# Reordering the last spans of each layer in a two-layer graph network kernel: late edge rows added by VectorE from SBUF, slot sums in one portion, block sums ahead of older blocks' stages, source one-hots earlier

## The chip, the cores and the metric

The kernel runs on one core of a Trainium2 chip. The metric is the device time of one execution in microseconds (us). Three runs of the kernel before took 2167.27, 2167.39 and 2170.34 us; their median is 2167.39.

## What is computed

Two graph layers over 6250 nodes and 106250 edges, rows of 256 float32. The edges are sorted by target node. Cut to what matters:

```python
# layer 0
msg = relu(x[src] + edge_attr)
h = 2 * x + segment_sum(msg, dst)
f = gelu(bn1(h) @ W1.T + b1) @ W2.T + b2
x1 = layernorm(x + bn2(h + f))
# layer 1
m = gelu((x1[src] + edge_attr) @ W1m + b1m) @ W2m + b2m
agg = segment_sum(m, dst) / max(deg, 1)
u = gelu(agg @ W1u + b1u) @ W2u + b2u
out = layernorm(x1 + layernorm(x1 + u) * gamma + beta)
```

The kernel adds 2x into a block's sum as a product with twice the identity. Layer 0's first product and layer 1's last message product work on block sums. Layer 1 gathers rows of `proj = x1 @ W1m + b1m`, so that the product with W1m is made once for each node, and once for each edge's own row.

## The kernel before

**Spans.** The edges are cut into 831 tiles of 128, and the tiles into 104 spans (0 to 103) of 8 (two groups of 4; a *quad* or pair is two tiles). For each span POOL gathers the source rows, one indirect DMA a tile (`gather`, L829), into one of five ring buffers. VectorE (DVE) adds the edge rows into the ring (`add_to_gathered`, L884), ScalarE (ACT) applies relu or gelu (L892, for pairs L898). TensorE (PE) then sums a span's edges into 128 *slots*: one-hots of the slot (L907, `one_hots`) times the rows, a PSUM bank named slotP of which there is one (L927, `slots_of`; `into_slots` does all 8 tiles, interleaved over four column groups). ACT copies the sums to SBUF (L946, `kept_slots`), and PE adds them into the node blocks they belong to (L966, `into_blocks`, with the degrees at L974).

**Blocks.** Node blocks have 256 nodes, and the last two 128 and 96; call them X and Y, and the last wide one A. When a block's last span has been added, its stages begin as a Python generator, one stage for each `advance`. In layer 0 (`nodes_0`) they are: copies out of the sum (begun by `full_0`); the first product (L1029) and gelu; the second product (L1042, L1047), the residual (L1052, L1054) and the statistics; square root (L1002), reciprocal (L1003) and scale (L1007), with the write of x1; transposes (L1066); the product with W1m (L1075, L1079) and the write of proj (L1084, for X and Y L1086). In layer 1 (`nodes_1`): residuals (L1331, L1335), the mean, the first product in two halves (L1357, L1362, L1367), the second product (L1378, L1382), a first norm (L1388, L1392) and the last norm with the write of the result. All use one PSUM bank named nodeP. `further()` advances every block that is running by one stage.

**Order.** The program is under a manual schedule: every engine runs its instructions in the order in which the Python code issues them, and waits for its operands there. So the order of calls in `step_0`, `step_1`, `late_step`, `end_0` and `end_1` is the order on each queue, the DMA queues of SP and POOL among them. `step_0(v)` gathers span v, adds the edge rows of span v-1 (first copied by ACT into PSUM, `lifted`, L867), and sums span v-2 into slots; `full_0(v-3)` adds the sums of span v-3 into blocks. The last four spans of each layer (100 to 103) go through `late_step` and `summed`. There the edge rows come to PSUM by PE, as products with an identity (`raised`, L875, 16 matmuls a span), and the slot sums are made in four portions of two tiles, with calls of `further()` between them.

**The turn.** Layer 1 can't gather from blocks that layer 0 hasn't finished. Its first three spans (AHEAD = 3; 24 gathers, from `src_near`) take only the rows of blocks up to A, and a blank row for a source in X or Y; all later gathers read the whole of proj. What the first three spans miss is put in by one-hots of the source: `where(i)` loads a copy of four tiles' source numbers to all partitions by a broadcast DMA (L1242, 256 KB) and compares them (DVE, L1250), and `completed` multiplies them with the rows of X and Y (PE, L1262). `added(v)` adds the first spans' edge part.

**The functions around the change** (`end_0` closes layer 0, `end_1` layer 1; before them `step_0` or `step_1` runs for spans 0 to 100, after `end_0` `step_1` begins):

Of the kernel before, what the change touches and what calls it, by code (L numbers as in the profile page):

```python
# [11 lines left out]
AF = mybir.ActivationFunctionType  # L12
# [3 lines left out]
D = 256  # L16
KC = D // P
G = 4
# [487 lines left out]
def kernel(  # L506
# [17 lines left out]
    nc = tc.nc  # L524
# [14 lines left out]
    ident = consts.tile([P, P], F32)  # L539
# [20 lines left out]
    col, at = {}, 0  # L560
    for name, n in COLS:
# [28 lines left out]
        ident=ident, ones=ones, eps=eps, col=col, row=row, src_sb=src_sb, dstf=dstf,  # L590
# [12 lines left out]
    V = len(window)  # L603
# [27 lines left out]
    def tiles_of(v, g):  # L631

        t0 = v * SPAN + g * G
        return [min(P, E - t * P) for t in range(t0, min(T, t0 + G))]

    def runs(counts):

        j = 0
        while j < len(counts):
            k = j  # L640
            while k < len(counts) and counts[k] == counts[j]:
                k += 1
            yield j, k, counts[j]
            j = k
# [3 lines left out]
    with (  # L648
# [17 lines left out]
        def work():  # L666
            return psw.tile([P, 2, D], F32, name="workP")
# [199 lines left out]
                nc.scalar.copy(ps[:n, j:k, :], of[:n, q + j : q + k, :])  # L867
            return ps

        def raised(v, g, q, of):  # L870

            pair = tiles_of(v, g)[q : q + 2]
            ps = work()
            for j, n in enumerate(pair):
                nc.tensor.matmul(  # L875
                    ps[:n, j, :], lhsT=ident[:n, :n], rhs=of[:n, q + j, :], start=True, stop=True
                )
            return ps

        def add_to_gathered(v, g, q, ps):  # L880
            at = g * G + q
            r = rings[v % RING]
            for j, k, n in runs(tiles_of(v, g)[q : q + 2]):
                nc.vector.tensor_add(  # L884
                    r[:n, at + j : at + k, :D], ps[:n, j:k, :], r[:n, at + j : at + k, :D]
                )
# [7 lines left out]
        def activated_pair(v, g, q, func):  # L894
            at = g * G + q
            for j, k, n in runs(tiles_of(v, g)[q : q + 2]):
                r = rings[v % RING][:n, at + j : at + k, :D]
                nc.scalar.activation(r, r, func)  # L898
# [37 lines left out]
        def into_slots(v, width):  # L936

            ps = slot_bank()
            count = len(tiles_of(v, 0) + tiles_of(v, 1))
            slots_of(v, width, ps, [j for i in range(PAIR) for j in range(i, count, PAIR)])  # L940
            return ps

        def kept_slots(v, ps, width):
            del hots[v]
            kept = hp.tile([P, D + 1], F32, name="sums")
            nc.scalar.copy(kept[:, :width], ps[:, :width])  # L946
            sums[v] = kept, ps
# [34 lines left out]
        running = []  # L982
# [106 lines left out]
        farther = []  # L1089
        eas, xbs, acc, degs = {}, {}, {}, {}  # L1090
# [68 lines left out]

        QUADS = [(g, q) for g in range(GROUPS) for q in range(0, G, 2)]  # L1160

        def summed(v, width, func, between=lambda i: None):

            one_hots(v)
            slot_nodes(v)
            its = [i for i in QUADS if tiles_of(v, i[0])[i[1] :]]
            rows = [raised(v, g, q, eas[v, g]) for g, q in its]
            for (g, q), ps in zip(its, rows):
                add_to_gathered(v, g, q, ps)
                activated_pair(v, g, q, func)  # L1170
            ps = slot_bank()
            for i, (g, q) in enumerate(its):
                between(i)
                at = g * G + q
                slots_of(v, width, ps, range(at, at + len(tiles_of(v, g)[q : q + 2])))
            kept_slots(v, ps, width)

        def further():
            advance(list(running))

        def late_step(v, full, func, width):

            u = v - 1
            if v == V - LATE:
                full(u - 2)
                activated(u - 1, 1, func)
                slot_nodes(u - 1)
                kept_slots(u - 1, into_slots(u - 1, width), width)
                further()
                full(u - 1)  # L1190
            summed(u, width, func, lambda i: further() if i % 2 else None)
            further()
            full(u)

        def kept_of(v):

# [38 lines left out]
        def added(v):  # L1235
            for g, q in QUADS:
                add_to_gathered(v, g, q, lifted(v, g, q, eas[v, g]))

        def where(i):

            to = check.tile([P, T], F32, name=("tiles", "off")[i % 2])[:, : G * P]
            nc.sync.dma_start(  # L1242
                out=to,
                in_=src_rows[i * G : (i + 1) * G, :].rearrange("t e -> (t e)")[None, :]
                .to_broadcast([P, G * P]),
            )
            hot = ep.tile([P, G, D], F32, name="z", bufs=2).rearrange("p g d -> p (g d)")
            hot = hot.rearrange("p (b e) -> p b e", e=G * P)
            for b in range(len(LAST)):
                nc.vector.tensor_scalar(  # L1250
                    hot[:, b, :], to, -float(near + sum(LAST[:b])), place,
                    op0=ALU.add, op1=ALU.is_equal,
                )
            wheres.append(hot)
# [13 lines left out]
        def end_0():  # L1268

            d = V - 1  # L1270
            for v in range(V - LATE, V):
                gather(v, x, src_sb)
                late_step(v, full_0, AF.Relu, D + 1)
            other = list(running)[-1]
            assert len(running) == 1 and len(farther) == 0
            for v in range(AHEAD):
                gather(v, proj[: near + 1, :], src_near)
                load_1(v)
            summed(d, D + 1, AF.Relu, lambda i: further() if i % 2 == 0 else None)
            full_0(d, acc_work)  # L1280
            last = list(running)[-1]
            assert len(running) == 2
            advance([last])
            for i in (0, 1):
                where(i)
            for _ in range(3):
                advance([other])
                advance([last])
            added(0)
            further()  # L1290
            further()
            assert not running and len(farther) == len(LAST)
            added(1)


# [156 lines left out]
        def full_1(v, bank=node_work, last=False):  # L1452
            for b in into_blocks(v, acc_1, opened_1):
                if last:
                    gen = prepared.pop(b)
                else:
                    gen = nodes_1(b, acc_1[b], x1s.pop(b), degs_1.pop(b), invs.pop(b), bank, last)
                del acc_1[b]
                begun(b, gen)
            invert()  # L1460
# [44 lines left out]
        def end_1():  # L1505

            d = V - 1
            for v in range(V - LATE, V):
                gather(v, proj, src_1)
                if v == V - 1:  # L1510
                    for b, bank in zip(sorted(acc_1), (node_work, acc_work)):
                        prepare(b, bank)
                late_step(v, lambda u: full_1(u, last=u == d - 1), AF.Gelu, D)
            assert len(running) == 1
            other = running[0]
            summed(d, D, AF.Gelu, lambda i: further() if i < 3 else None)
            full_1(d, last=True)
            last = running[-1]
            advance([last])
            advance([last])  # L1520
            while running:
                advance(list(running))
# [23 lines left out]
    other = nc.values_load(astray_i[:1, :1], min_val=0, max_val=2 * P)  # L1546
# [57 lines left out]
```

## Time and profile before

| What | Value |
|---|---|
| median of the runs shown | 2167.39 us (2167.27 to 2170.34) |
| the profiled execution | 2165.82 us, of which span 2163.9 us |
| mean granted TensorE clock | 0.968 |
| busy: PE, DVE, ACT, POOL | 1903.9, 1451.8, 1341.3, 1583.8 us |
| stretch 1010 to 1064: PE, DVE, ACT, POOL busy | 49.74, 27.61, 21.06, 30.11 of 54.00 us |
| stretch 2080 to 2160: PE, DVE, ACT, POOL busy | 59.01, 45.84, 33.13, 26.35 of 80.00 us |
| last gather of layer 0 ends | 1047.1 us |
| write of A's rows of proj issued (L1084) | 1058.85 us |
| first gather of layer 1 / first from the whole of proj | 1061.84 / 1094.94 us |
| identity groups (L875) start, layer 0 | 1020.73, 1035.61, 1049.64, 1061.01 us |
| identity groups (L875) start, layer 1 | 2086.67, 2099.76, 2120.15, 2133.50 us |
| block sums (L966) of spans 100 to 103 start, layer 1 | 2098.78, 2117.30, 2132.40, 2146.93 us |

The times are from one execution, taken by the hardware profiler, counted from the span's start. PEclk is the share of its full clock that TensorE was granted. A timeline row gives the start, the duration, the engine, the line and the operation, and in brackets how long the engine had been idle before, and what ended that. The chain of waits is the work that ended last, followed back from the last instruction to what released it. A row of a windows table gives for one stretch the busy time of each engine, the number of its instructions in parentheses, the granted clock, the DMA engines' share and the rate.

### The profile page before, as it was taken

To read this page: it belongs to the slowest core of one execution; us is meant where nothing else is said; L and a number is where in the kernel's file an instruction comes from. 1 tells how busy PE (TensorE), PEld (TensorE's weight loads), DVE (VectorE), ACT (ScalarE), POOL (GpSimd) and SP (SyncE) were. 2 spreads that over 40 slices of the span, in tenths; PEclk is the share of its full clock that TensorE was granted. 3 is DMA by queue.
4 is the path that set the end of the run, shared out by engine and by line. 5 is a ranking of instruction groups with operands and counts; after the bars stand their busy time and mean duration, and the time that the engine had idled before them with its cause. 6 is when DMAs were issued, how large, how long until landed. Compare 5 with 4: busy or idle time off the path is not lost.

```text
span 2163.9 us, 38059 instructions
## 1 busy us (share of the span) xinstructions
PE 1903.9 (88%) x12071; PEld 1472.0 (68%) x12071; DVE 1451.8 (67%) x4205; ACT 1341.3 (62%) x2153; POOL 1583.8 (73%) x1671
## 2 busy tenths in 40 slices
PE   5999999998998989898779998898888988888886
PEld 3777767776776777666557776677766766766654
DVE  6677766776776667666366766676676766666665
ACT  3577766676766666665336766665665666666653
POOL 7777777777777777777567777777777777777770
PEclk9999999999999999999989999999999999999998
DMA  9889888888988898887568777777777767777650
GB/s 335 263 290 323 293 294 290 292 287 286 301 289 283 287 295 281 286 288 243 174 206 267 225 244 233 221 238 243 227 227 228 242 213 235 219 233 227 212 167 26
DMA packets 318430, 541.75 MB, mean 250 GB/s; under 512 B 37260, under 2 KB 234125, under 8 KB 318093
## 3 DMA queue, kind: packets, MB, share of 16 engines
q1 hardware_dynamic: 237773, 319.65, 44.3%
q0 software_dynamic: 79744, 217.71, 32.6%
q8 instruction: 99, 1.62, 0.3%
q10 hardware_dynamic: 704, 1.87, 0.2%
q14 instruction: 110, 0.90, 0.1%
HBM read 461.90 MB, written 77.18 MB: 249 GB/s over the span
## 4 chain that ended last, share of the span: by engine, by line
PE 21%; DMA 12%; DVE 8%; issue 6%; ACT 4%; POOL 3%; DVEq 0%; ACTq 0%; POOLq 0%
DMA ring<-proj,dst_sb 11%; PE workP L856 8%; POOL ring L829 3%; PE slotP L927 3%; DVE ring L884 2%; PE nodeP L1378 2%; PE acc L966 2%; PE nodeP L1357 2%; DVE hot L907 2%; PE workP L843 1%; DVE uT L1362 1%; ACT ring L892 1%; ACT L1002 1%; PE workP L1262 1%; ACT workP L867 1%
## 5 line engine op out<-in xcount | busy, mean ns | idle before, releaser
L829 POOL DMA_INDIRECT ring<-in_x_dram,src_sb x831 | 789.0, 949 | 255.6 <-issue 137.3
L829 POOL DMA_INDIRECT ring<-proj,dst_sb x807 | 769.9, 954 | 252.8 <-issue 152.3
L856 PE MATMUL workP<-w1m_sb,eaT 128*128 128x256 f32 x3324 | 830.0, 395 | 67.8 <-DVE ring L884 45.4
L884 DVE TENSOR_TENSOR ring<-workP,ring 128x512 f32<-128x512 f32 x844 | 557.2, 684 | 426.8 <-DMA ring<-in_x_dram,src_sb 126.0
L856 PEld LDWEIGHTS workP<-w1m_sb,eaT 128*128 128x128 f32 x3324 | 621.1, 195 | 237.2 <-DVE ring L884 58.3
L892 ACT ACTIVATE ring<-ring 128x1024 f32<-128x1024 f32 x400 | 424.8, 1062 | 147.7 <-DVE ring L884 144.7
L848 ACT COPY eaT<-workP 128x512 f32<-128x512 f32 x416 | 223.8, 585 | 262.7 <-PE workP L843 261.6
L867 ACT COPY workP<-ea 128x512 f32<-128x512 f32 x606 | 334.0, 595 | 32.0 <-DVE ring L884 30.6
L966 PE MATMUL acc<-hot,sums 128*128 128x161 f32 (+22 forms) x1376 | 225.1, 296 | 91.5 <-DVE hot L960 48.9
L907 DVE TENSOR_SCALAR hot<-ramp,slot 128x32 f32<-128x32 f32 x1662 | 268.1, 259 | 0.2 <-PE slotP L927 0.2
L966 PEld LDWEIGHTS acc<-hot,sums 128*128 128x128 f32 x1376 | 187.0, 195 | 110.6 <-DVE hot L960 53.9
L927 PE MATMUL slotP<-ring,hot 128*32 128x257 f32 (+1 forms) x3324 | 248.6, 388 | 12.0 <-ACT ring L892 6.2
L843 PE MATMUL workP<-ident,ea 128*128 128x128 f32 x1584 | 212.3, 276 | 15.8 <-DMA ea<-in_edge_attr_dram 8.6
L843 PEld LDWEIGHTS workP<-ident,ea 128*128 128x128 f32 x1584 | 186.2, 142 | 41.1 <-issue 10.6
L927 PEld LDWEIGHTS slotP<-ring,hot 128*32 128x32 f32 x3324 | 97.7, 109 | 129.2 <-issue 63.3
L946 ACT COPY sums<-slotP 128x257 f32<-128x257 f32 (+1 forms) x208 | 75.4, 362 | 134.4 <-PE slotP L927 134.4
L1367 ACT ACTIVATE uT<-uT,cols_sb 128x256 f32<-128x256 f32 (+3 forms) x104 | 45.8, 487 | 132.5 <-DVE uT L1362 132.4
L1357 PE MATMUL nodeP<-fT,w 128*128 128x256 f32 (+2 forms) x400 | 101.5, 400 | 25.6 <-DVE y L1392 25.2
L1357 PEld LDWEIGHTS nodeP<-fT,w 128*128 128x128 f32 x400 | 77.9, 204 | 45.6 <-DVE y L1392 32.1
L1002 ACT ACT_TABLE_LOAD x73 | 93.7, 1283 | 1.3
L1378 PE MATMUL nodeP<-w2u_sb,uT 128*128 128x256 f32 (+1 forms) x392 | 89.3, 381 | 1.4 <-DVE y L1335 1.4
L1156 DVE COPY z<-workP 128x512 f32<-128x512 f32 x101 | 69.1, 684 | 20.7 <-PE workP L856 20.0
(154 smaller groups left out, 1582.5 us busy)
## 6 DMA issues: line engine op xcount, KB each, us to landing
ea<-in_edge_attr_dram SPq DMA_DIRECT2D x103, 1024.0 KB
ea<-zst SPq DMA_DIRECT2D x110, 512.0 KB
zst<-z SPq DMA_DIRECT2D x101, 512.0 KB
ea<-in_edge_attr_dram SPq DMA_DIRECT2D x97, 512.0 KB
ring<-in_x_dram,src_sb POOLq DMA_INDIRECT x831
ring<-proj,dst_sb POOLq DMA_INDIRECT x807
xb<-in_x_dram SPq DMA_DIRECT2D x23, 256.0 KB
x1d<-x SPq DMA_DIRECT2D x23, 256.0 KB
```

Of the source, the lines that this page charges most:

```text
L829: nc.gpsimd.indirect_dma_start(out=rings[v % RING][:n, j, :D], out_offset=None, in_=table, in_offset=bass.IndirectOffsetOnAxis(ap=rows[:n, ...
L843: nc.tensor.transpose(pe[:, j, k, :n], ea[:n, at + j, k * P : (k + 1) * P], ident[:n, :n])
L848: nc.scalar.copy(eaT[:, j:k, :, :n], pe[:, j:k, :, :n])
L856: nc.tensor.matmul(ph[:n, j, :], lhsT=eaT[:, j, k, :n], rhs=w1m_sb[:, k, :], start=(k == 0), stop=(k == KC - 1),)
L867: nc.scalar.copy(ps[:n, j:k, :], of[:n, q + j : q + k, :])
L884: nc.vector.tensor_add(r[:n, at + j : at + k, :D], ps[:n, j:k, :], r[:n, at + j : at + k, :D])
L892: nc.scalar.activation(at, at, func)
L907: nc.vector.tensor_scalar(hots[v][:n, j, :], ramp[:n, :SLOTS], slot[:n, t : t + 1], None, op0=ALU.is_equal,)
L927: nc.tensor.matmul(ps[q * SLOTS : (q + 1) * SLOTS, :width], lhsT=hot[:n, j, :], rhs=r[:n, j, :width], start=(i == 0), stop=(i == PAIR - 1 ...
L966: nc.tensor.matmul(acc[b][:, k, cols], lhsT=its[:, k * P : (k + 1) * P], rhs=at, start=(begins and k == 0), stop=(last_span[b] == v and k ...
L1357: nc.tensor.matmul(ps[:, o - i, :width], lhsT=w12[:, k, o * P : (o + 1) * P], rhs=mT[:, k, :width], start=(k == 0), stop=(k == KC - 1),)
L1378: nc.tensor.matmul(ps[:n, h, :], lhsT=uT[:, k, h * n : (h + 1) * n], rhs=w2u_sb[:, k, :], start=(k == 0), stop=(k == UC - 1),)
```

## The change

`raised` and its identity products go: in `summed`, VectorE adds each pair's edge rows to the ring with both operands in SBUF, and ACT's activation of the pair follows at once. The slot sums are made in one portion by `into_slots`, after a single call of `between`. `late_step` adds a span's sums to the blocks right after they are kept, and runs up to three rounds of the running blocks' stages behind that; before, these rounds lay between the portions. In `end_0`, `where(0)` and `where(1)` move from behind block Y's beginning to the front of the function, ahead of the late spans; `added(0)` moves from ahead of the last two rounds of stages to behind them. In `end_1`, `prepare` (the residuals of X and Y) keeps its place in the program, written now behind the second late step instead of ahead of the third, and one stage of X's lies ahead of span 103's slot sums, where there were three among the portions. The number of instructions on DVE, ACT, SP and POOL stays; PE has fewer by the identity products.

```diff
-        def raised(v, g, q, of):
-            pair = tiles_of(v, g)[q : q + 2]
-            ps = work()
-            for j, n in enumerate(pair):
-                nc.tensor.matmul(
-                    ps[:n, j, :], lhsT=ident[:n, :n], rhs=of[:n, q + j, :], start=True, stop=True
-                )
-            return ps
...
-        def summed(v, width, func, between=lambda i: None):
+        def summed(v, width, func, between=lambda: None):
             one_hots(v)
             slot_nodes(v)
-            its = [i for i in QUADS if tiles_of(v, i[0])[i[1] :]]
-            rows = [raised(v, g, q, eas[v, g]) for g, q in its]
-            for (g, q), ps in zip(its, rows):
-                add_to_gathered(v, g, q, ps)
-                activated_pair(v, g, q, func)
-            ps = slot_bank()
-            for i, (g, q) in enumerate(its):
-                between(i)
-                at = g * G + q
-                slots_of(v, width, ps, range(at, at + len(tiles_of(v, g)[q : q + 2])))
-            kept_slots(v, ps, width)
+            for g, q in QUADS:
+                its = tiles_of(v, g)[q : q + 2]
+                if its:
+                    add_to_gathered(v, g, q, eas[v, g][:, q : q + 2, :])
+                    activated_pair(v, g, q, func)
+            between()
+            kept_slots(v, into_slots(v, width), width)
...
                 activated(u - 1, 1, func)
                 slot_nodes(u - 1)
                 kept_slots(u - 1, into_slots(u - 1, width), width)
+                full(u - 1)
+            summed(u, width, func)
+            full(u)
+            for _ in range(3 if v + 1 < V else 1):
                 further()
-                full(u - 1)
-            summed(u, width, func, lambda i: further() if i % 2 else None)
-            further()
-            full(u)
...
         def end_0():
             d = V - 1
+            for i in (0, 1):
+                where(i)
             for v in range(V - LATE, V):
                 gather(v, x, src_sb)
                 late_step(v, full_0, AF.Relu, D + 1)
...
-            summed(d, D + 1, AF.Relu, lambda i: further() if i % 2 == 0 else None)
+            summed(d, D + 1, AF.Relu)
             full_0(d, acc_work)
...
             advance([last])
-            for i in (0, 1):
-                where(i)
             for _ in range(3):
                 advance([other])
                 advance([last])
-            added(0)
-            further()
             further()
             assert not running and len(farther) == len(LAST)
+            added(0)
             added(1)
...
             for v in range(V - LATE, V):
                 gather(v, proj, src_1)
-                if v == V - 1:
+                late_step(v, lambda u: full_1(u, last=u == d - 1), AF.Gelu, D)
+                if v == d - 1:
                     for b, bank in zip(sorted(acc_1), (node_work, acc_work)):
                         prepare(b, bank)
-                late_step(v, lambda u: full_1(u, last=u == d - 1), AF.Gelu, D)
...
-            summed(d, D, AF.Gelu, lambda i: further() if i < 3 else None)
+            (other,) = running
+            summed(d, D, AF.Gelu, further)
             full_1(d, last=True)
```

More of the change, by code (lines that the diff above doesn't have):

```diff
@@ L1273, in end_0 @@
                 late_step(v, full_0, AF.Relu, D + 1)
-            other = list(running)[-1]
-            assert len(running) == 1 and len(farther) == 0
+            (other,) = running
+            assert len(farther) == 0
             for v in range(AHEAD):
@@ L1278, in end_0 @@
                 load_1(v)
-            summed(d, D + 1, AF.Relu, lambda i: further() if i % 2 == 0 else None)
+            summed(d, D + 1, AF.Relu)
             full_0(d, acc_work)
-            last = list(running)[-1]
-            assert len(running) == 2
+            last = running[-1]
             advance([last])
-            for i in (0, 1):
-                where(i)
             for _ in range(3):
@@ L1509, in end_1 @@
                 gather(v, proj, src_1)
-                if v == V - 1:
+                late_step(v, lambda u: full_1(u, last=u == d - 1), AF.Gelu, D)
+                if v == d - 1:
                     for b, bank in zip(sorted(acc_1), (node_work, acc_work)):
                         prepare(b, bank)
-                late_step(v, lambda u: full_1(u, last=u == d - 1), AF.Gelu, D)
-            assert len(running) == 1
-            other = running[0]
-            summed(d, D, AF.Gelu, lambda i: further() if i < 3 else None)
+            (other,) = running
+            summed(d, D, AF.Gelu, further)
             full_1(d, last=True)
```

## The prediction

> **What bounds the kernel now.** I read the page first, then POOL's timeline, then the chain of waits, then windows of the two tails.
>
> ```profile
> PE 1903.9 (88%) x12071; PEld 1472.0 (68%) x12071; DVE 1451.8 (67%) x4205; ACT 1341.3 (62%) x2153; POOL 1583.8 (73%) x1671
> L829 POOL DMA_INDIRECT ring<-in_x_dram,src_sb x831 | 789.0, 949 | 255.6 <-issue 137.3
> ```
>
> PE is busiest, but POOL sets the pace: a gather (0.95) and 0.30 of issue are 1.25 us, 8 a span are 10 us, and in layer 0 they run from 4.85 to 1047.1 without a stop. The only stops are in POOL's timeline:
>
> ```profile
> 1061.84 0.98 POOL L829 DMA_INDIRECT ring<-proj,src_near  x1 [14.75 <-DMA degd<-degs]
> 1094.94 0.94 POOL L829 DMA_INDIRECT ring<-proj,dst_sb  x1 [3.05 <-DMA proj<-y]
> 1098.06 0.94 POOL L829 DMA_INDIRECT ring<-proj,dst_sb  x1 [2.18 <-PE workP L1262]
> ```
>
> Layer 1's gathers need layer 0's results. The 24 near gathers (30 us) wait for block A's rows (write issued 1058.85, first gather 3.0 later); the far ones for blocks X and Y (issued 1091.59, gather 3.35 later). From there the stream runs to 2114.6, and the last spans' work follows to 2163.9. So the time is set at two places, the turn (1010 to 1100) and the end (2080 to 2164). All the change's edits lie there. The chain of waits at the end holds two identity matmul groups:
>
> ```profile
> 2086.83 3.47 PE workP L875 x16
> 2120.36 4.83 PE workP L875 x16
> ```
>
> Together 8.3 us. The second took 4.83 because the clock was halved, as windows of 3.41 us show (columns: stretch, its length, busy PE, PEld, DVE, ACT, POOL, PEclk, DMA share, GB/s):
>
> ```profile
> 2099.07:2102.49 3.42, 3.42 (x21) 3.12 (x21) 2.16 (x7) 2.54 (x3) 2.50 (x4) 1.00 0.39 115
> 2102.49:2105.90 3.41, 0.91 (x5) 0.45 (x3) 3.34 (x16) 0.00 (x0) 2.80 (x3) 1.00 0.39 113
> 2105.90:2109.32 3.42, 2.47 (x6) 1.07 (x7) 2.03 (x4) 3.13 (x5) 2.51 (x4) 0.50 0.36 99
> 2109.32:2112.73 3.41, 3.41 (x10) 2.19 (x10) 1.28 (x4) 2.15 (x3) 2.50 (x4) 0.50 0.45 139
> 2116.14:2119.56 3.42, 1.25 (x8) 0.73 (x6) 2.06 (x6) 1.97 (x5) 0.00 (x0) 1.00 0.01 2
> 2119.56:2122.97 3.41, 3.41 (x11) 2.88 (x11) 2.97 (x13) 0.37 (x1) 0.00 (x0) 0.50 0.00 0
> ```
>
> A window with 0.91 or 1.25 of PE work is followed by one at 0.50; one with 2.47 does not bring the clock back, one with 3.41 does. At half clock L1357's 8 matmuls take 3.78 instead of 2.0, about 1.85 times. Other rows put the bound near 45% (1.61 and 1.85 of 3.41 were followed by half clock). This decides my forecast: the change takes PE work away and lays the rest end to end with other engines' work.
>
> **Part 1, VectorE adds straight from SBUF.** It removes 4 identity groups a layer from PE: 3.72 each, 3.38 the last, 5.04 and 4.85 at half clock. The adds stay, 4 a span, 2.47 together (0.684 each). No late add from two SBUF tiles is in the trace; the nearest rows:
>
> ```profile
> L798 DVE TENSOR_TENSOR w2s_sb<-w2t_sb,bn_s x2: 417/418/418, 33.2 to 33.7; 128x256 f32<-128x256 f32 x2
> 50.51 1.02 DVE L748 TENSOR_TENSOR off<-off 128x831 f32<-128x831 f32 x1
> ```
>
> 418 ns for 128x256 from SBUF against 432 at L1052 with a PSUM operand; L748, scaled to 512 columns, 0.63. So an add costs 0.63 to 0.70, over 16 a layer -0.9 to +0.3 us. I take 0.684: nothing.
>
> The adds may hold up POOL beside them: gathers at 49.21, 50.97 and 52.65 took 1.45, 1.38 and 1.39, among DVE's operations on SBUF at 48.8 to 54.3. At +0.45 for each gather that meets an add (at most 8 a layer) that is 0 to 3.6 us a layer, taken at 0: before the near gathers POOL waits 14.75 us anyway, and at the end the stream stops before the last adds.
>
> The Trainium skill ("SBUF — State Buffer", section "Who interferes with whom") says that a VectorE instruction with two SBUF inputs contends with a GpSimd instruction that reads SBUF, and infers that descriptor generation needs the write side, so a tensor_tensor should not stall it. That would make this term 0. The slow gathers lay among two-input and one-input forms alike, so this trace does not separate them.
>
> **Part 2, one portion.** Before, four portions of 2 tiles (1.05 each, PE L927) with stages of older blocks between; now 8 tiles in one run over 4 column groups, 1.07 (as at 2112.41, 8 in 1.20). 3 us of PE go, but the stages that lay between go behind the block sums.
>
> **Part 3, block sums ahead of stages.** full() of a span comes right after its sums (0.37), then up to three rounds of stages before the next span's one-hots in DVE's order. The three after full(100) hold stages 3 to 5 of the block before A (call it Z) and 2 to 4 of A, and are a serial chain, since nodeP has one buffer: Z's L1042 and L1047 2.95 and DVE's two adds that free nodeP 1.4; A's L1029 2.0, table load and gelu 2.1, L1042 and L1047 2.95, DVE's adds 1.4 and statistics 1.2, sqrt with reciprocal and table load 1.75, scale 0.74: 16.5, and 18 in the layout with the hand-offs between engines. The adds, being behind them on DVE, no longer lie beside PE's stage work. Who waits: span 101's one-hots (1.53), adds (2.47), relu (0.64), portion, sums; then block A's last two stages, and POOL.
>
> **Part 4, the source one-hots earlier.** Two 256 KB loads (SP) and four DVE operations move from behind block Y's start to the front of the tail:
>
> ```profile
> 1081.62 0.88 DVE L1250 TENSOR_SCALAR z<-tiles,place 128x512 f32<-128x512 f32 x2 [8.22 <-DMA tiles<-src_rows]
> ```
>
> That 8.22 us idle goes. On SP the loads now follow the write of z at 1012.8, ahead of later loads which POOL does not wait for. At the same latency (issued 1073.13, used 8.49 later) they are usable at about 1021.3, and DVE is stuck till then, with full(99)'s sums and span 100's one-hots queued behind. Bounds: 0 if they land in DVE's idle stretch (1014.93 to 1019.25), 8.2 at most. I take +2.7: DVE idles to 1021.3, spends 1.1 more, and one-hots that began at 1022.31 begin near 1025.
>
> **Sum at full clock.** Laid out the same way, the kernel before comes out 2 us late at both places, so I trust differences. After: A's write issued at 1061.6 instead of 1058.85 (+2.7), near gathers from 1064.6 to 1094.6; X's and Y's writes at 1086.7 and 1087.7 (before 1087.98 and 1091.59) land before that, so the far gathers start at 1094.6 (-0.3), and the adds for spans 0 and 1 end 1.4 earlier. At the end full(100) is at 2090.3 (before 2098.8), full(101) 2114.6 (2117.3), full(102) 2137.6 (2132.4), full(103) 2145.8 (2146.9), last scale +0.8: the 8.3 us saved on the chain are spent waiting for stages. In all about -0.5.
>
> **Sum at the clock that the rows give.** In the end's last 73 us PE has 32.7 us of work instead of 55.5, a share of 45%; at the turn 20.9 between 1022 and 1061 and 13.1 from there to 1089, all of it on the path. Applying "under 45% busy halves the next window, 84% brings it back", half clock covers 1020 to 1037, 1051 to 1061, 1072 to 1078 and 1082 to 1092: A's write +6.8 more, far gathers +6 and adds +8 against the same layout of before. I take **+7** at the turn. At the end half clock covers five stretches, last scale +9 (the phase of the windows makes it 9 to 14); since that rule is drawn from few rows, I take **+7**. 2165.82 (span 2163.9 plus 1.9) + 14 = 2179.8; the median lies 1.57 above this execution: **2181**.
>
> The Trainium skill ("TensorE: Matmul & The Clock Gate", Part 1) says that a window which is idle brings half clock and a busy one full clock. Were only a nearly idle window to count, the end would cost about +5 and the turn about +6; this trace's windows at 0.91 to 1.85 speak against it.
>
> **Rivals.** (1) *PE keeps its clock.* For: the tails' mean clock is 0.97 and 0.90 now. Against: the rows above. 2165.8 - 0.5 + 1.6 = 2167; with the lower bounds of parts 1 and 4 (-1.8 and -2.7) 2162, with the upper ones half used 2171. (2) *The cuts come through, faster.* The 8.3 us on the chain and the far wait of 3.05 go, as stages run beside adds: 2165.8 - 11.4 + 1.6 = 2156. It decides if the three rounds take under 12 us instead of 18, since A's write must come 6 us sooner. Against: each round's sqrt and scale stand ahead of the one-hots on DVE. (3) *Half clock nearly throughout, gathers held up besides.* All PE work on the path at 1.85 would add 17.8 at the turn and 27.8 at the end; half of the way from nothing, 14 each with the hold-up: 2195.
>
> **Chances.** Forecast 0.60, from 2171 (+2 at each place) to 2193 (the end's +14 instead of +7, and the load's bound of 8.2 instead of 2.7), rival 1 0.20, rival 2 0.13, rival 3 0.07. The range leaves out 2 and 3: 2162 to 2193. A measurement here can tell about 0.2%, 4.3 us. Faster: rival 2 and a little of rival 1, 0.14; same: most of rival 1, 0.18; slower 0.68.
>
> **What would show it.** Right: 0.50 windows after 1020 and in the end, PE busy under 1.6 ahead of them; A's write near 1066; last full() near 2150 or later; DVE idle at L1250 gone from 1073 and 6 us of it near 1015. Wrong: A's write before 1060, clock 1.00 through both tails, or gathers over 1.2 us beside the adds.

## The result, and the profile after

The changed kernel takes 2188.16 us (median of 6 runs, 2186.52 to 2194.59), the kernel before 2167.33 (6 runs): ratio 1.0099, 95% interval 1.0084 to 1.0114. It is slower by 21 us, where +14 was forecast. The ratios leave out runs that took over 1.5% more than the fastest of their kernel; where runs spread by more (e5 to e12), the medians of all runs are given beside them. The profiled execution took 2187.11 us, its span 2185.3, the mean clock 0.951 instead of 0.968.

The page of the changed kernel (its lines are lower in number than before, by 10 at the first and some 16 at the last: the adds are L874, the slot sums L917, the block sums L956):

```profile
PE 1894.8 (87%) x11947; PEld 1460.7 (67%) x11947; DVE 1450.6 (66%) x4205; ACT 1334.2 (61%) x2147; POOL 1587.2 (73%) x1671
...
L829 POOL DMA_INDIRECT ring<-in_x_dram,src_sb x831 | 791.0, 952 | 255.8 <-issue 137.4
```

PE's busy time fell by 9 us only, though the identity products that went took 31.7 (124 products at L875): what is left ran some 22 us longer. VectorE, ACT and POOL did what they did before, but for six fewer loads of ACT's function table (2147 instead of 2153 instructions; ahead of the prediction the number is said to stay). Nothing on the page tells of 21 us; they are in the two tails. POOL's stops, from its timeline:

```profile
1072.88 1.66 POOL L829 DMA_INDIRECT ring<-proj,src_near  x1 [23.63 <-issue]
...
1108.51 0.94 POOL L829 DMA_INDIRECT ring<-proj,dst_sb  x1 [2.01 <-PE workP L1248]
...
1139.24 0.94 POOL L829 DMA_INDIRECT ring<-proj,dst_sb  x1 [1.79 <-issue]
```

The wait for block A's rows grew from 14.75 to 23.63, the wait of 3.05 for X and Y is gone, and the last gather starts at 2122.47 instead of 2113.71. Counting along the gathers, from the starts and ends of POOL's rows:

| Part | before | after | difference |
|---|---|---|---|
| first near gather starts | 1061.84 | 1072.88 | +11.04 |
| from there to the first far gather: near gathers longer | | | +2.32 |
| the wait ahead of the first far gather, over the usual 0.30 | 2.75 | 0.00 | -2.75 |
| first far gather to last gather | 1018.77 | 1016.92 | -1.85 |
| start of last gather to end of last scale | 44.88 | 57.48 | +12.60 |
| end of last scale | 2158.59 | 2179.95 | +21.36 |

So about +9 comes from the turn and +12.6 from the end.

**The turn.** VectorE's and PE's timelines of the changed kernel:

```profile
1018.27 0.88 DVE L1236 TENSOR_SCALAR z<-tiles,place 128x512 f32<-128x512 f32 x2 [5.16 <-DMA tiles<-src_rows]
1020.88 0.88 DVE L1236 TENSOR_SCALAR z<-off,place 128x512 f32<-128x512 f32 x2 [1.73 <-DMA off<-src_rows]
...
1028.36 1.35 DVE L897 TENSOR_SCALAR hot<-ramp,slot 128x32 f32<-128x32 f32 x8
```

```profile
1022.03 2.04 PE L917 MATMUL slotP<-ring,hot 128*32 128x257 f32 x16 [7.02 <-DVE degs L969]
1024.55 1.20 PE L956 MATMUL acc<-hot,sums 128*128 128x112 f32 x4 [0.48 <-ACT sums L936]
...
1061.23 3.78 PE L1065 MATMUL nodeP<-w1m_sb,fT 128*128 128x256 f32 x8
```

VectorE stands for the source numbers for 6.9 us (the second load is in use at 1020.88, forecast 1021.3), PE is idle 7.02 behind it, and then comes back at half clock: 16 slot sums take 2.04 (1.56 at the same place before), the last product of block Z 3.78. Z's took 3.59 before, at half clock too, but at 1030.85, long ahead of A's last; now A's (1.99, at 1067.18) follows directly behind it. Span 100's one-hots begin 6.05 later than before (1022.31), A's write is issued at 1069.93 (before 1058.85). The windows around it (columns as in the prediction):

```profile
1013.90:1017.30 3.40, 1.11 (x7) 0.56 (x6) 0.00 (x0) 1.78 (x3) 2.62 (x3) 1.00 1.07 368
1017.30:1020.70 3.40, 0.00 (x0) 0.00 (x0) 0.88 (x2) 0.00 (x0) 2.66 (x3) 0.51 0.77 247
1020.70:1024.10 3.40, 2.04 (x16) 0.88 (x16) 1.63 (x5) 0.00 (x0) 2.48 (x4) 0.50 0.35 106
```

PE busy 1.11 of 3.40, and the next window is granted half.

**The end.** The chain of waits of the changed kernel, in place of the identity products at 2086.83 and 2120.36:

```profile
2105.90 3.79 PE nodeP L1341 x8
...
2134.92 6.37 PE nodeP L1362 x16
2141.32 0.70 DVE hT L1366
...
2167.42 3.57 PE acc L1341 x16
```

Products of the stages stand on it at half clock: L1341's 8 take 3.79 (L1357 before, 2.0 at full clock), L1362's 16 take 6.37 (L1378 before, 3.72). Between the two, PE's rows have one more L1341 at half clock (2113.00, 3.67) and an L1362 at full clock (2117.64, 3.72). VectorE shows the order:

```profile
2121.39 0.69 DVE L1366 TENSOR_TENSOR hT<-nodeP,hT 128x512 f32<-128x512 f32 x1 [3.81 <-PE nodeP L1362]
...
2124.38 1.25 DVE L897 TENSOR_SCALAR hot<-ramp,slot 128x32 f32<-128x32 f32 x8
```

The block sums of span 100 start at 2099.44, the one-hots of span 101 only at 2124.38, behind three rounds of stages. Before, these came at 2098.78 and 2104.07.

PE's work done in windows at half clock, from PE's rows and the clock's: up to the first near gather 3.4 us before and 19.9 after; from 2080 on 12.7 and 28.2. At 1.85 times its length such work loses 46%: at most 1.6 and 9.1 us, and 5.8 and 13.0 (upper bounds, since not all of this work lies on the path). So half clock makes at most 9.1 of the turn's +11.04. At the end it can make up to 13.0, less what the kernel before loses in the same way.

How much of the end's work at half clock lies on the path, the chains of waits tell, as an estimate. In the changed kernel, from span 100's block sums on, 21.6 us of products and block sums ran at half clock on it, which is 9.9 lost, or 13.0 with the slot sums, which also wait for ACT; in the kernel before 3.3, or 4.3. So some 7 to 9 of the end's +12.6 are the clock's, and the other 4 to 6 the order's at any clock.

The stages of the end, from the starts of the block sums in both kernels and in the forecast:

| From, to | before | forecast at full clock | measured |
|---|---|---|---|
| block sums of span 100, of span 101 | 18.52 | 24.3 | 31.63 |
| of span 101, of span 102 | 15.10 | 23.0 | 26.15 |
| of span 102, of span 103 | 14.53 | 8.2 | 9.07 |
| of span 103, end of the last scale | 11.66 | 13.6 | 13.66 |

Up to span 100's block sums the new order gains: they come 0.66 later than before, though the gathers are 8.76 late. Behind them it loses 20.7: 13.1 with the three rounds ahead of span 101 and 11.1 with those ahead of span 102, 5.5 come back ahead of span 103, and 2.0 go behind it.

### The profile page after: what moved, and what is told of

The parts are those of the page before. It is cut to its first block, busy times and chain, and to the rows that moved or that the text cites. A ratio compares the mean times of both kernels' runs of the same rounds, so it can differ in the third digit from the quotient of the medians.

```text
span 2185.3 us, 37776 instructions
## 1 busy us (share of the span) xinstructions
PE 1894.8 (87%) x11947; PEld 1460.7 (67%) x11947; DVE 1450.6 (66%) x4205; ACT 1334.2 (61%) x2147; POOL 1587.2 (73%) x1671
## 3 DMA queue, kind: packets, MB, share of 16 engines
q0 software_dynamic: 79744, 217.71, 31.7%
## 5 line engine op out<-in xcount | busy, mean ns | idle before, releaser
L874 DVE TENSOR_TENSOR ring<-workP,ring 128x512 f32<-128x512 f32 x812 | 538.4, 684 | 434.1 <-DMA ring<-in_x_dram,src_sb 138.0
L956 PE MATMUL acc<-hot,sums 128*128 128x161 f32 (+22 forms) x1376 | 231.7, 302 | 90.8 <-DVE hot L950 51.5
L917 PE MATMUL slotP<-ring,hot 128*32 128x257 f32 (+1 forms) x3324 | 250.0, 395 | 49.2 <-ACT ring L888 35.7
L956 PEld LDWEIGHTS acc<-hot,sums 128*128 128x128 f32 x1376 | 192.0, 199 | 112.7 <-DVE hot L950 56.2
L843 PEld LDWEIGHTS workP<-ident,ea 128*128 128x128 f32 x1584 | 188.9, 144 | 40.8 <-issue 10.3
L917 PEld LDWEIGHTS slotP<-ring,hot 128*32 128x32 f32 x3324 | 96.1, 110 | 170.7 <-issue 61.2
L1341 PE MATMUL nodeP<-fT,w 128*128 128x256 f32 (+2 forms) x400 | 102.1, 402 | 30.6 <-DVE y L1376 25.6
L1341 PEld LDWEIGHTS nodeP<-fT,w 128*128 128x128 f32 x400 | 78.8, 206 | 50.5 <-DVE y L1376 32.4
L1362 PE MATMUL nodeP<-w2u_sb,uT 128*128 128x256 f32 (+1 forms) x392 | 92.0, 389 | 3.7 <-DVE y L1376 2.7
L969 DVE TENSOR_TENSOR degs<-degs,slotP 1x161 f32<-1x161 f32 (+25 forms) x172 | 36.5, 240 | 73.4 <-PE slotP L964 16.2
```

The lines of the kernel that those rows point to most:

```text
L843: nc.tensor.transpose(pe[:, j, k, :n], ea[:n, at + j, k * P : (k + 1) * P], ident[:n, :n])
L874: nc.vector.tensor_add(r[:n, at + j : at + k, :D], ps[:n, j:k, :], r[:n, at + j : at + k, :D])
L917: nc.tensor.matmul(ps[q * SLOTS : (q + 1) * SLOTS, :width], lhsT=hot[:n, j, :], rhs=r[:n, j, :width], start=(i == 0), stop=(i == PAIR - 1 ...
L956: nc.tensor.matmul(acc[b][:, k, cols], lhsT=its[:, k * P : (k + 1) * P], rhs=at, start=(begins and k == 0), stop=(last_span[b] == v and k ...
L1341: nc.tensor.matmul(ps[:, o - i, :width], lhsT=w12[:, k, o * P : (o + 1) * P], rhs=mT[:, k, :width], start=(k == 0), stop=(k == KC - 1),)
L1362: nc.tensor.matmul(ps[:n, h, :], lhsT=uT[:, k, h * n : (h + 1) * n], rhs=w2u_sb[:, k, :], start=(k == 0), stop=(k == UC - 1),)
```

## The experiments

Theory: the loss is half clock, which comes because PE has less work and has it end to end with other engines' work. Rivals: the order itself (a round of stages ahead of the next span's one-hots costs at any clock); the early source one-hots; the adds from SBUF in themselves. Not taken apart were the other parts of the order: one portion, block sums ahead of the stages, the place of `added(0)`.

The first four ran together, against 2169.62 us for the kernel before (15 runs).

### e1: the adds alone

```diff
-            rows = [raised(v, g, q, eas[v, g]) for g, q in its]
-            for (g, q), ps in zip(its, rows):
-                add_to_gathered(v, g, q, ps)
+            for g, q in its:
+                add_to_gathered(v, g, q, eas[v, g][:, q : q + 2, :])
                 activated_pair(v, g, q, func)
```

> The kernel before with the identity products alone replaced by adds from SBUF; four portions, order and the source one-hots as before. If the loss of the change comes from the order (stages end to end behind the block sums), this kernel is free of it and gains what PE sheds: the 8.3 us of identity products on the end's chain and up to 7.4 us at the turn (two groups of 3.72 ahead of block A's write), so 2153 to 2162. If it comes from PE being left with too little work for its clock, this kernel has it too: 0.50 windows in both tails and 2165 to 2180.

Measured: 2179.18 us, ratio 1.0037 (1.0025 to 1.0050). Taking the identity products off PE, with nothing else changed but the adds' operands, makes the kernel slower. The clock fell to 0.954, and PE's work at half clock rose from 3.4 to 11.0 at the turn and from 12.7 to 18.5 at the end. That is what the clock theory expected. But the trace shows a second cause, on POOL and VectorE:

```profile
2091.60 0.95 POOL L829 DMA_INDIRECT ring<-proj,dst_sb  x1 [0.30 <-issue]
2092.85 3.17 POOL L829 DMA_INDIRECT ring<-proj,dst_sb  x1 [0.30 <-issue]
2096.32 0.95 POOL L829 DMA_INDIRECT ring<-proj,dst_sb  x1 [0.31 <-issue]
```

```profile
2092.71 2.49 DVE L874 TENSOR_TENSOR ring<-ea,ring 128x512 f32<-128x512 f32 x4
```

A gather that begins inside the four adds lasts until 0.82 us after the last of them. The same is seen in the changed kernel: adds 1029.75 to 1032.23, gather 1030.01 to 1033.05. In e1 four gathers were held so, two of them at the turn's beginning (2.96 and 2.69), one among the near gathers (2.60), one at the end (3.17); in the kernel before, whose adds take one operand from PSUM, the gather is not held. Its POOL and VectorE at span 100:

```profile
1023.71 0.95 POOL L829 DMA_INDIRECT ring<-in_x_dram,src_sb  x1 [0.30 <-issue]
1024.96 0.95 POOL L829 DMA_INDIRECT ring<-in_x_dram,src_sb  x1 [0.30 <-issue]
```

```profile
1023.69 2.46 DVE L884 TENSOR_TENSOR ring<-workP,ring 128x512 f32<-128x512 f32 x4
```

Two gathers begin inside the run of adds, and both take 0.95. How the +8 divides between clock and held gathers, e5, e9 and e12 were to tell. e1's own trace, whose execution took 7.0 us more than the profiled one before, gives an estimate. The two gathers at the turn's beginning lie ahead of a wait of POOL of 14.3 us, and the one at 2092.85 belongs to span 101, whose adds come only at 2112.32. Only the near one (1065.64) stands on the chain of waits, 1.65 us longer than usual. So the held gathers make at most some 2 of the 7 us.

### e2: the order alone

The changed kernel with `raised` back (the three lines with "-" above, ahead of the one portion).

> The changed kernel with the identity products back in front of the adds: order, one portion and early source one-hots as changed, PE's work as before. If the clock decides, the 0.50 windows of the tails shrink to those of the kernel before and the time falls below the changed kernel's 2188, to 2172 to 2182, though the products lie on the path again. If the order decides, the products come on top of it (two of them, 7 to 8 us, on the path): 2190 to 2198.

Measured: 2181.19 us, ratio 1.0050 (1.0034 to 1.0066). By the ratios the loss is about half of the changed kernel's (1.0099), though 13 us of products lie on its chain of waits again (5.49 ahead of the near gathers, 4.51 and 3.23 at the end): so far the clock theory. But the windows did not shrink to those of the kernel before, as it had it: at half clock PE did 9.1 us up to the first near gather, but 25.2 from 2080 on. PE's timeline of e2 at the end:

```profile
2118.53 3.62 PE L875 MATMUL workP<-ea,ident 128*128 128x256 f32 x16
2124.50 2.84 PE L927 MATMUL slotP<-ring,hot 128*32 128x256 f32 x16 [2.35 <-ACT ring L898]
2127.86 1.13 PE L966 MATMUL acc<-hot,sums 128*128 128x120 f32 x8 [0.52 <-ACT sums L946]
2131.72 6.66 PE L1372 MATMUL nodeP<-w2u_sb,uT 128*128 128x256 f32 x16 [2.73 <-DVE y L1386]
2138.21 3.62 PE L875 MATMUL workP<-ea,ident 128*128 128x256 f32 x16
2150.08 3.71 PE L927 MATMUL slotP<-ring,hot 128*32 128x256 f32 x16 [8.26 <-ACT ring L898]
```

With the work of before, PE still waits 8.26 us in one piece, since the order puts it there. The adds alone cost 8 us and the order alone 11, and both together 21: within their intervals, of about 3 us each, they add up.

### e3: the source one-hots back at their old place

```diff
-            for i in (0, 1):
-                where(i)
             for v in range(V - LATE, V):
...
             advance([last])
+            for i in (0, 1):
+                where(i)
```

> The changed kernel with the first source one-hots back at their old place. The changed kernel's VectorE stood till 1021.7 for them and its one-hots of span 100 began at 1028.36, 6.05 later than before. If that wait is a cost of the early place, A's write comes about 6 us sooner than 1070, the old wait of 8.2 at the same place comes back between A's write and those of X and Y, and the time falls by 0 to 6: 2182 to 2188. If the early place was a gain, as the 8.2 us idle suggests, the time rises to 2190 to 2196.

Measured: 2192.14 us, ratio 1.0108 (1.0093 to 1.0123); the changed kernel's interval reaches to 1.0114. No difference that can be told, though the time itself lies in the range that was given for a gain. In the profiled execution, the fastest of the five (2182.64), A's write is issued at 1059.03 instead of 1069.93, about as early as before the change (1058.85): so the early place, with the half clock that follows it, cost 10.9 us there and not 6. The wait ahead of the near gathers is 10.40 instead of 23.63, but the wait ahead of the far ones is 7.12, and PE does 23.5 us at half clock between the two (14.8 in the changed kernel). The wait moved from one place to the other, and most of what A's write gained was lost again: the far gathers begin 3.7 us sooner (1101.81 instead of 1105.55). The place neither gains nor costs a time that the medians can tell.

### e4: matmuls that nobody reads

```diff
+        def kept_busy(count):
+            ps = work()
+            for i in range(count):
+                nc.tensor.matmul(ps[:, i % 2, :], lhsT=ident, rhs=w1t_sb[:, 0, :], start=True, stop=True)
...
+            kept_busy(16)
             for g, q in QUADS:
...
             between()
+            kept_busy(4)
...
             for gen in which:
+                if late:
+                    kept_busy(4)
```

> The changed kernel with matmuls that nobody reads added to PE in both tails: 16 ahead of each late span's adds, 4 ahead of its slot sums, 4 ahead of each stage; the result is the reference's. Waits between engines stay as changed; only PE's clock and its queue differ. If half clock makes the loss, the granted clock rises from 0.951 towards 0.97 or more and the time falls to 2168 to 2178 (the added work itself costs up to 0.9 us for each group that is late). If the order alone makes it, the time stays at 2186 to 2195 at a full clock.

Measured: 2236.18 us, ratio 1.0306 (1.0292 to 1.0320). The clock came: the mean is 0.966, and at the end it was full. The time rose by 45 to 48 us, and both theories missed. The windows of e4, the turn and the end (its last gather starts at 2159.70, 37 us later than in the changed kernel), then of the changed kernel:

```profile
1010.00:1100.00 90.00, 78.74 (x427) 63.52 (x426) 29.83 (x92) 20.32 (x35) 39.95 (x40) 0.91 0.32 100
2126.00:2226.00 100.00, 95.31 (x517) 80.27 (x516) 41.03 (x126) 28.18 (x53) 26.66 (x27) 1.00 0.15 44
```

```profile
1010.00:1100.00 90.00, 57.71 (x273) 36.73 (x262) 35.91 (x111) 28.20 (x53) 51.74 (x50) 0.75 0.46 150
2080.00:2164.00 84.00, 48.02 (x212) 30.44 (x210) 45.55 (x136) 29.85 (x52) 32.98 (x35) 0.78 0.24 74
```

e4's chain of waits shows where the time went (L876 are the added matmuls):

```profile
2160.96 10.36 PE workP L876 x48
...
2181.01 13.81 PE workP L876 x64
```

From 2130.41 to 2226.89 the added matmuls take 67.5 of the 96.5 us of the chain: up to 64 run one after another, and the kernel's own work stands behind them on PE. The expectation, up to 0.9 us for each group, was far too low. So this experiment does not separate clock from order: it says only that a full clock bought in this way costs more than it gives.

### e5 to e12, beside longer transfers

From here on the chips moved data more slowly (190 GB/s in the mean on e5's page, 250 on that of the kernel before): the kernel before itself took 2806 to 2859 us beside them (page of e5, POOL's gathers):

```profile
L829 POOL DMA_INDIRECT ring<-proj,dst_sb x807 | 766.8, 950 | 598.1 <-issue 273.6
L829 POOL DMA_INDIRECT ring<-in_x_dram,src_sb x831 | 789.0, 949 | 536.1 <-issue 237.9
```

A gather takes what it took (950), but POOL is idle 598.1 and 536.1 us ahead of them instead of 252.8 and 255.6. So ratios stand against the kernel before of the same call, and their intervals are wide.

e5, e9 and e12 are one kernel, the kernel before with the adds from SBUF and the products still made, but unused:

```diff
             rows = [raised(v, g, q, eas[v, g]) for g, q in its]
-            for (g, q), ps in zip(its, rows):
-                add_to_gathered(v, g, q, ps)
+            for g, q in its:
+                add_to_gathered(v, g, q, eas[v, g][:, q : q + 2, :])
```

> The kernel before with the adds taken from SBUF and the identity products still made, but read by nobody (the result is the reference's): PE's work is that of the kernel before, VectorE's that of the adds-only kernel (ratio 1.0037). If the adds-only kernel lost time because PE's clock fell, this one has the clock of before (0.968) and is level with it or a little faster, since the adds wait for no product: ratio 0.996 to 1.001. If adding from SBUF itself costs (slower adds, gathers held up), it is as slow as the adds-only kernel or slower: 1.003 to 1.006.

> The kernel of e5 again, for a measurement where the kernel before takes its 2167 to 2170. PE's work is that of the kernel before, VectorE's that of the adds-only kernel (ratio 1.0037). Clock theory: ratio 0.996 to 1.001, half clock in the tails as in the kernel before. Adds from SBUF cost in themselves: 1.003 to 1.006.

> The kernel of e5 and e9 once more, to be measured where the kernel before takes its 2167 to 2170. PE does the work of the kernel before, VectorE that of the adds-only kernel, whose +8 us (ratio 1.0037) may come from PE's clock or from gathers that begin beside the adds and then last 2.6 to 3.2 us instead of 0.95. If the clock makes all of it, ratio 0.996 to 1.000. If the held-up gathers make it, 1.002 to 1.005, with a last gather about 2 us longer for each run of adds that meets one. If both, in between.

Measured: 1.0042 (1.0001 to 1.0083), 0.9989 (0.9945 to 1.0034), 0.9929 (0.9890 to 0.9969). By the medians of all runs the ratios are 0.9997, 1.0011 and 0.9927. The first answer lies in the range of costly adds, the second in that of the clock, the third below both, and the first moves into the clock's range by the medians. The traces show that only one gather of a kernel began inside the adds here (2.60 or 2.61, ending 0.49 after the last add, which is short). So the three do not tell how much of e1's +8 is clock and how much held gathers; no run settles it, and the estimate from e1's trace is all there is.

e6 and e10 are e2 with the adds from SBUF and the products unused:

> The changed kernel with the identity products made ahead of each late span's adds and read by nobody. It differs from the order-only kernel (2181.2, ratio 1.0050) only in that the adds do not wait for them, and from the changed kernel (ratio 1.0099) only by PE's extra work, 25 products a layer's tail or more. If the clock makes a part of the loss, the extra work brings time back: ratio 1.002 to 1.005. If the identity work has no other effect than to stand on PE's queue, it costs: 1.010 to 1.014.

> The kernel of e6 again, for the same reason. Clock theory: the extra work of PE brings time back against the changed kernel (1.0099), and the adds wait for no product as in the order-only kernel (1.0050): 1.002 to 1.005. If the identity work only stands on PE's queue: 1.010 to 1.014.

Measured: 1.0040 (1.0005 to 1.0075) and 1.0003 (0.9971 to 1.0034), by the medians of all runs 1.0018 and 1.0004: lower than the changed kernel's 1.0099, as the clock theory had it, but that one was measured beside shorter transfers, so it is a hint and no more. The traces don't support it either: from 34 us ahead of the last gather on, PE does 28.3 and 31.0 us at half clock, about as much as in e8 and e11 below, which have no such products at the end (29.2 and 32.4).

e7 is the kernel before with the two loads at the front of the tail and the compares left in place:

```diff
+            for i in (0, 1):
+                where_load(i)
             for v in range(V - LATE, V):
```

> The kernel before with the two loads of source numbers issued at the front of the tail and their compares left at the old place. Nothing waits for the loads then: VectorE's 8.22 us idle at 1081.62 falls under 1, the writes of X and Y come up to 8 us earlier, and the far gathers' wait of 3.05 goes; what follows it (2.18 and 2.68) may take its place. If the wait was worth its length past the near gathers: ratio 0.996 to 0.9985. If the clock, with PE's idle time gone at 1076, decides: 0.994 to 0.997. If another wait takes its place: 0.999 to 1.001.

Measured: 1.0062 (1.0022 to 1.0103), outside all three. In this trace POOL waits 42.57 us ahead of the near gathers and 19.34 ahead of the far ones, which are other waits than those of 2167 us; whether the split gains there was not measured.

e8 and e11 are one kernel, the turn as before and the end as changed (`end_1` calls the new `late_step` and `summed`, `end_0` the old ones):

> The turn as before, the end as changed (late steps and span 103 of layer 1 alone take the new form). In the profile of the changed kernel the last gather is 8.8 us later than before and the last VectorE instruction 21.4, so 12.6 of the loss lie behind the last gather. If the two places are independent, this kernel takes 10 to 14 us more than before: ratio 1.0046 to 1.0065. If the end's loss came with the shifted phase of the turn, it is under 1.003.

> The kernel of e8 again, for the same reason: the turn as before, the end as changed. If the two places are independent, it takes the 12.6 us which the changed kernel lost behind its last gather: ratio 1.0046 to 1.0065. If the end's loss came with the shifted phase of the turn, it is under 1.003.

Measured: 1.0057 (1.0015 to 1.0099) and 1.0050 (1.0021 to 1.0079), both in the range of independent places. But both intervals reach below 1.003, and by the medians of all runs the ratios are 1.0025 and 1.0042, so the times alone don't decide. The traces do, and they agree across all kernels. From the end of the last gather to the end of the last scale:

| order at the end | before at 2167 to 2170 us | before at 2806 to 2859 us |
|---|---|---|
| of before | 44.0 (before), 46.8 (e1) | 75.5, 85.4, 76.0 (e5, e9, e12), 83.5 (e7) |
| changed | 56.6 (after), 55.7 (e2), 54.9 (e3) | 90.6, 90.4 (e8, e11), 93.7, 93.8 (e6, e10) |

With or without the products, with the source one-hots early or late, every kernel with the changed order lies above every one with the order of before: by 10.3 us in the means of the first column (55.7 against 45.4) and 12.0 in those of the second (92.1 against 80.1). So the changed end costs by itself, whatever the turn does. PE's work at half clock there (counted as in e6 and e10) goes the same way: 12.7 and 18.5 us with the order of before against 24.5 to 28.2 in the first column, 15.6 to 22.5 against 28.3 to 32.4 in the second.

## Why the prediction was right, and where its terms were off

**The direction and the mechanism held.** PE's clock falls in both tails, after windows in which it has little to do, and the loss of 21 lies in the range. The clock's rule was rougher than I took it: 1.46 of 3.40 at 2119.90 was followed by a full clock, one with 1.80 of 3.41 at 1037.82 too, and a window of 3.40 at 1058.30 by another half one. Of the rows that the bound near 45% was drawn from, 1.85 of 3.41 is itself 54%: the bound lies nowhere sharply. A length of 3.78 instead of 2.0 is 1.89 times, not 1.85. The Trainium skill ("TensorE: Matmul & The Clock Gate", Part 1) has half clock follow an idle window; here also windows with 1.11 of 3.40 (1013.90) and 0.63 (1048.10) were followed by it, so the measured rows stand against reading "idle" as empty.

**The turn, +7 forecast, +8.8 measured at the last gather.** A's write: forecast +2.7 at full clock and +6.8 from the clock, 1068.4; measured 1069.93, with at most 9.1 from the clock and the rest from VectorE's stand; with the source one-hots back at their old place (e3) it came at 1059.03. The early loads: the time at which they came was right, but not what stood behind them; full(99) ran at half clock, so the one-hots were 6.05 late and not 2.7. The far wait went, as forecast.

**Gathers held up, forecast 0, measured +2.32 among the near gathers.** This term was mis-sized. I bounded it by 0.45 for each gather from rows at 49 to 53, and took 0 since POOL waits there anyway. One held gather costs 2 us (3.04, 2.92 instead of 0.95). Gathers over 1.2 us beside the adds were named as a sign of being wrong, and they came. Two of the four runs of adds in layer 0 fell after the wait, when the near gathers were on the path. The Trainium skill ("SBUF — State Buffer", "Who interferes with whom") infers that a tensor_tensor should not stall descriptor generation; the gathers that began inside runs of adds from two SBUF tiles and ended 0.82 to 0.86 us after a full run show that such adds do hold an indirect gather, and the measurement decides. Whether they hold its descriptors is not shown: a gather also takes its row numbers from SBUF (`src_sb`), and the section's other sentence, on GpSimd instructions that read SBUF, would fit that.

**The end, +7 forecast, +12.6 measured.** The term that was too small is the clock's. The layout at full clock held up to span 100's block sums (8.1 gained, 8.5 forecast). Behind them the measured stages took 11.4 us more than this layout (80.5 against 69.1), most of it, 7.3, in the three rounds ahead of span 101; and products at half clock on the path lost 10 to 13 in the whole stretch. The clock's rule had +9 to +14, and I took +7. Nor does "+0.8" mean that the order is nearly free: it stands against a kernel before that itself loses 3 to 4 us to half clock, and with both freed of that loss the order costs some 4 to 6 (the estimate above). No experiment separates the two; e4 was to do it and could not. One saving was not there: the slot sums in one portion took 2.9 to 4.3 us in the late spans of both layers that have them in one row of PE's, in part at half clock, and not 1.07, since the products of a pair begin only when ACT has done the pair. That the total (21 against 14) still lies in the range owes something to its width.

**Rivals.** The kernel that keeps its clock did not occur in any order-changed kernel without added work. The faster one needed three rounds in under 12 us; from the block sums of span 100 to the one-hots of span 101 they took 25 us at the end (2099.44 to 2124.38) and 15.7 at the turn (1035.22 to 1050.87, forecast 18). Gathers held up, part of the third rival, came true at a few us, but the clock was not half nearly throughout (43 of 95 us at the end).

## What to carry to other kernels

Work that is taken off an engine that isn't waiting for it can still make the kernel slower, if that work kept the engine's clock up, or if what replaces it holds up another engine's transfers: look at the stretch's busy share and at what else uses SBUF before counting a saving. Where an engine runs in program order, a stage put "behind" the block sums of one span is put ahead of the next span's one-hots; count the whole round there, not only its matmuls.

## What the runs showed of the hardware

- A gather (indirect DMA issued by POOL) that begins inside a run of VectorE adds with both operands in SBUF, or up to 0.24 us ahead of it, lasts until that run is over: it ended 0.82 to 0.86 us after runs of full adds and 0.48 or 0.49 after runs that end in a 10-row add, and took up to 3.54 us instead of 0.95 (e3, at 1019.68). With one operand in PSUM, the 438 gathers that began beside adds in the kernel before took 0.95 in the median and 1.05 at most. There are exceptions: in one run of e1 (2112.32) a gather of 1.19 ended inside the run, and beside a single add a gather that began 0.07 ahead took 0.95 (changed kernel, 2093.71). Why is open.
- Adding from SBUF itself is not slower: four adds take 2.48, with a PSUM operand 2.47.
- Removing the identity products of the tails (3.4 to 3.7 us for each of eight spans at full clock) lowered the mean clock: it was 0.949 to 0.957 in e1's runs and 0.960 to 0.966 in those of the kernel before beside them. The time rose by 0.37%, held gathers being a part of it.
- TensorE's clock fell to half after windows of 3.4 us with up to 1.85 us of matmuls and stayed full after others with 1.46 or 1.80, so between these the busy share alone did not tell the next window's clock.
